# Banded attention in layer 1: softmax sums in eight tiles of 64 by 32, their reciprocal in three parts

## The chip, the core and the metric

The kernel runs on one core of a Trainium2 chip. A core has five engines that run side by side: TensorE (PE in the profile; its weight loads are shown apart as PEld), VectorE (DVE), ScalarE (ACT), GpSimd (POOL) and SyncE (SP), which here issues the transfers. The metric is the device time of one execution in microseconds, as the median of several runs. Lower is better.

## What is computed

Two layers follow each other on an image `x` of 128 rows of 256 tokens of 256 channels, all in fp32. Each normalizes by groups, attends within each row, and adds its input. Layer 0 has eight heads of 32 channels, a gate and a bias behind the softmax. The change lies in layer 1, which has four heads of 64 channels and lets a token see only the tokens at most 16 away:

```python
qkv = x2 @ w_in.T + b_in
q, k, v = map(heads, jnp.split(qkv, 3, axis=-1))        # 4 heads of 64 channels
scores = jnp.einsum('bhid,bhjd->bhij', q, k) / jnp.sqrt(D)
scores = jnp.where(jnp.abs(i - j) <= 16, scores, -jnp.inf)
attn = jax.nn.softmax(scores, axis=-1)
out = jnp.einsum('bhij,bhjd->bhid', attn, v)
y = out.reshape(...) @ w_out.T + b_out
```

## The kernel before

One image row of 256 tokens is a sample; there are S = 128 samples in 64 pairs. Layer 1 keeps channels on the partitions and tokens along the free side. The tokens are cut into NB = 4 blocks of KB = 64 keys; a block of keys meets a window of 96 queries at most. The four heads are numbered by `half` (0 or 1) and `j` (0 or 1). The keys of the heads of half 0 lie on partitions 0 to 63, those of half 1 on partitions 64 to 127 of the same tile, so that TensorE can be used as four tiles of 64 by 64: rows by `half`, columns by `j`.

The softmax isn't divided out before the product with v. The exponentials go into a banded tile `p`, and POOL adds its two rows of blocks into `zp` (L1085), in which the sum over the 64 partitions of a half is the softmax's sum of each of the 256 queries. `attend` (L1088 to L1122) does for a pair, sample r = 0 and then r = 1:

- 16 products of `p` with v into `av` (L1107), in tiles of 64 by 64;
- 4 products of `zp` with a matrix `place` into `zs` (L1117), also in tiles of 64 by 64. `place` has ones in 16 of its 64 columns, other ones for each half and sample, so that the sums of 2 halves and 2 samples gather on different groups of 16 partitions. Sample 0 starts the accumulation in PSUM and sample 1 ends it; each half has its own PSUM bank.

Each fp32 product shows in the profile as two matmuls (two passes). `sums` (L1124) then adds the two banks: ACT copies one (L1129), DVE adds the other (L1130). `inverse` takes the reciprocal on DVE (L1141) in two parts of 128 columns. `by_transfer` writes one row of each group of 16 partitions to DRAM (L1149, two transfers) and reads it back spread over 64 partitions each (L1153, two transfers) into `near`; SP issues all four. `divide` multiplies `av` by `near` on DVE (L1173), which gives `at`. The last two pairs use two products with `spread` (L1164) in place of the transfers.

Layer 1's loop runs over pairs i in an order written out by hand for all engines: scores of pair i; output transposes and stores of pair i - 3 (`finish`); `attend`, `sums` and the first part of `inverse` for pair i - 1; then `stretch(i + 1, i - 2)`, the projections; then normalization of pair i + 2 (on ACT; its helper also has SP issue the load of a later pair's `yg`), `divide(i - 1)`, the row sums of `at` on POOL, the least of the sums on DVE (`bounds`), and the values v of pair i + 1 (L1047).

`stretch` runs three streams at once: q and k of pair i + 1, and the output projection o of pair i - 2. Each has seven products n, made in the order 2, 1, 5, 6, 7, 4, 3 (a scheme with seven products in place of eight); `in_turn` (L687 to L700) goes round the three streams for each n. Behind each product the stream's bank is emptied (`take`): for q and k mostly by ACT (L666, L668), for o by DVE (L662), and the additions L675, L681, L685 by DVE. A stream has one PSUM bank, so its next product waits for the take. Behind product 1 of all three streams, `amid` puts the second part of the reciprocal and the transfers into the order.

Of the kernel before, what the change touches and what calls it, by code (L numbers as in the profile page):

```python
# [39 lines left out]
def conv_preact_kernel(  # L40
# [59 lines left out]
    def strip(a):  # L100
        return slice(B * a, B * (a + 1))
# [582 lines left out]
            elif n == 3:  # L684
                nc.vector.tensor_tensor(to[:, 2], ps[:, 1, :], self.mid, ALU.add)  # L685

    def in_turn(sevens, amid=lambda: None):  # L687


        for p in sevens:  # L690
            p.open()

            p.product(2, p.ps[:, 1, :], first=True)
            p.take(2)
        for n in (1, 5, 6, 7, 4, 3):
            for p in sevens:
                p.product(n)
                p.take(n)
            if n == 1:
                amid()  # L700

    def one_by_one(w, at, name, done):

# [19 lines left out]
    with ExitStack() as both:  # L723
# [20 lines left out]
        with ExitStack() as lay0:  # L744
# [140 lines left out]
            def stretch(names, i, s, rest=lambda: None):  # L885

                po = iter(())
                if s >= 0:
                    po = one_by_one(out_sb, st[s]["at"], f"po{s}", lambda ps: st[s].update(po=ps))
                if 2 * i >= S:  # L890
                    rest()
                    for _ in po:
                        pass
                    return
                f, g = (
                    Seven(row, quarters[w], xns[i], tss[i], f"{w}{i}", w, by_token=(w == "v")) for w in names
                )
                for w, p in zip(names, (f, g)):
                    res[w, i] = p.to
                two_of_them(row, f, g, f"{names}{i}", po, rest)  # L900
# [70 lines left out]
        with ExitStack() as lay:  # L971
# [4 lines left out]

            weights = [att.tile([P, 2, 2 * WROW], F32, name=f"1p{i}", bufs=1) for i in range(4)]

            place = att.tile([P, 2, D1], F32, name="place", bufs=1)
            nc.gpsimd.memset(place, 0.0)  # L980
            for half in range(2):
                for r in range(2):
                    c = 32 * half + 16 * r
                    nc.gpsimd.memset(place[KB * half : KB * (half + 1), r, c : c + 16], 1.0)

            spread = att.tile([P, 2, 2, P], F32, name="spread", bufs=1)
            for half in range(2):
                for r in range(2):
                    nc.gpsimd.tensor_copy(
                        spread[:, half, r].rearrange("p (j d) -> p j d", j=2),  # L990
                        ident[:, 32 * half + 16 * r :: D1].unsqueeze(2).to_broadcast([P, 2, D1]),
                    )
            xns, tss = {}, {}

# [26 lines left out]

            ats, ats_t, outputs, last_ots = {}, {}, {}, {}

            def stretch(i, j, amid=lambda: None):


                streams = [
                    Summed(row, quarters1[w], xns[i], tss[i], f"1{w}{i}", w, bias=bqk[:, 0:2] if w == "q" else None)
                    for w in "qk"
                ]  # L1030
                f, g = streams
                if j >= 0:
                    outputs[j] = Summed(row, quarters1["o"], ats[j], ats_t[j], f"1o{j}", "out", bias=bo_v, y=ygs[j])
                    streams.append(outputs[j])
                in_turn(streams, amid)
                for r in range(2):
                    st[2 * i + r].update(q=f.to[:, 2 * r : 2 * r + 2, :], k=g.to[:, 2 * r : 2 * r + 2, :])
# [50 lines left out]
            def attend(i):  # L1088

                if i < 0:  # L1090
                    return

                if i < S // 2 - 1:
                    av = ps_av.tile([P, 2, 2, R], F32, tag="av", name=f"1av{i}", bufs=1)
                    av = [av[:, half] for half in range(2)]
                else:
                    av = [proj_bank(f"1av{i}_{half}") for half in range(2)]
                zs = ps_av.tile([P, 2, 2, R], F32, tag="zs", name=f"1zs{i}", bufs=1)
                for r in range(2):
                    (p, zp), v = hd.pop(2 * i + r), st[2 * i + r]["v"]  # L1100
                    for b in range(NB):
                        for half in range(2):
                            for j in range(2):
                                keys, cols = slice(KB * half, KB * (half + 1)), slice(D1 * j, D1 * (j + 1))
                                q0, p0 = QLO[b], R * (b % 2) + QLO[b]

                                nc.tensor.matmul(  # L1107
                                    av[half][cols, r, q0 + QIN[b].start : q0 + QIN[b].stop],
                                    lhsT=v[keys, b, cols],
                                    rhs=p[keys, j, p0 + QIN[b].start : p0 + QIN[b].stop],  # L1110
                                    start=(r == 0 and b == 0), stop=(b == NB - 1),
                                    skip_group_check=True,
                                )
                    for half in range(2):
                        for j in range(2):
                            keys, cols = slice(KB * half, KB * (half + 1)), slice(D1 * j, D1 * (j + 1))
                            nc.tensor.matmul(  # L1117
                                zs[cols, half, 0, :], lhsT=place[keys, r, :], rhs=zp[keys, j, :],
                                start=(r == 0), stop=(r == 1),
                                skip_group_check=True,  # L1120
                            )
                hd["av", i] = (av, zs)  # L1122

            def sums(i):  # L1124
# [7 lines left out]
                near = att.tile([P, 2, 2, R], F32, tag="near", name=f"1near{i}", bufs=1)  # L1132
                hd["z", i] = (z, rz, near)

            def inverse(i, part):

                if i < 0:
                    return
                z, rz, _ = hd["z", i]
                cols = slice(P * part, P * (part + 1))  # L1140
                nc.vector.reciprocal(rz[:, cols], z[:, cols])  # L1141

            def by_transfer(i):

                if i < 0:
                    return
                _, rz, near = hd["z", i]
                for j in range(2):
                    nc.sync.dma_start(  # L1149
                        out=rz_far[i % 2, j], in_=rz[D1 * j : D1 * (j + 1)].rearrange("(n c) q -> n c q", c=16)[:, 0, :]  # L1150
                    )
                for j in range(2):
                    nc.sync.dma_start(  # L1153
                        out=near[D1 * j : D1 * (j + 1)].rearrange("p h r q -> p (h r q)"),
                        in_=rz_far[i % 2, j].rearrange("n q -> (n q)").partition_broadcast(D1),
                    )

            def by_product(i):

                _, rz, near = hd["z", i]  # L1160
                for half in range(2):
                    ps = proj_bank(f"1near{i}_{half}")
                    for r in range(2):
                        nc.tensor.matmul(ps[:, r, :], lhsT=spread[:, half, r], rhs=rz, start=True, stop=True)  # L1164
                    nc.scalar.copy(near[:, half], ps)

            def divide(i):
                if i < 0:
                    return
                ats[i] = row.tile([P, 4, R], F32, tag="at", name=f"1at{i}", bufs=2)  # L1170
                av = hd.pop(("av", i))[0]
                for half in range(2):
                    nc.vector.tensor_tensor(ats[i][:, half::2], av[half], hd["z", i][2][:, half], ALU.mult)  # L1173
                for r in range(2):
                    st[2 * i + r]["at"] = ats[i][:, 2 * r : 2 * r + 2, :]

# [63 lines left out]
            with tc.manual_schedule(engines={  # L1240
# [12 lines left out]
                for i in range(last):  # L1253
                    s = 2 * i
                    scores(s)
                    scores(s + 1)
                    finish(i - 3)
                    attend(i - 1)
                    sums(i - 1)
                    inverse(i - 1, 0)  # L1260

                    def amid():
                        inverse(i - 1, 1)
                        by_transfer(i - 1)

                    stretch(i + 1, i - 2, amid)
                    normal(i + 2, True)
                    divide(i - 1)
                    if 0 <= i - 1 < last - 2:
                        ats_t[i - 1] = row.tile([P, 4, R], F32, tag="att", name=f"1att{i - 1}", bufs=2)  # L1270
                        row_sums(ats_t[i - 1], ats[i - 1], nc.gpsimd)
                    bounds(i - 1)
                    values(s + 2)
                    values(s + 3)
# [15 lines left out]
                sums(last - 1)  # L1290
                for s in (S - 6, S - 5):
                    all_of(s)
                for part in range(2):
                    inverse(last - 1, part)
                by_product(last - 1)
                for s in (S - 6, S - 5):
# [1 line left out]
                attend(last)  # L1298
                sums(last)
                divide(last - 1)  # L1300
                for part in range(2):
                    inverse(last, part)
                all_of(S - 4)
                by_product(last)
# [214 lines left out]
```

## Time and profile before

| what | value |
|---|---|
| median of 3 runs | 3195.79 us (3195.11 to 3196.19) |
| the profiled execution | 3194.72 us, span from its first to its last instruction 3193.0 us |
| mean granted TensorE clock | 0.993 |
| busy PE / PEld | 3115.2 us (98%) / 2404.0 us (75%) |
| busy DVE / ACT / POOL | 2536.9 us (79%) / 1868.3 us (59%) / 1609.2 us (50%) |
| one pass of layer 1's loop | 16.79 us, PE's start of v to the next one |
| reciprocal of the sums, L1141, 128x128 | 947 ns, 124 times |
| products of the sums, L1117 | 1024 recorded matmuls |
| division, L1173 | 686 ns, waits 53.7 us in all for `1near` |

A span is divided among the engines by their busy time, but matmuls are pipelined and their ends are modelled: two that overlap are not each a cost, so PE's cost is read from the distance between starts. A line of a timeline gives start, length over all that were merged, engine, source line, operation, output and inputs, for a matmul the tile of the array (rows by columns) and the shapes, the count, and in brackets how long the engine had been idle and who ended that. DVE's instructions overlap by some 0.08 us when they follow each other without a wait.

### The profile page before, as it was taken

What the parts mean: (1) busy time and instruction counts of PE and PEld (TensorE: products, weight loads), DVE (VectorE), ACT (ScalarE), POOL (GpSimd) and SP (SyncE); (2) the same over time, 40 slices, a digit from 0 to 9 for tenths busy, and PEclk for the clock granted to TensorE, in tenths of its full rate; (3) what the DMA queues carried; (4) which work ended last, traced back from release to release, by engine and by line L of the source; (5) the groups of instructions that cost most, each with busy time, mean ns of one, the idle gap of its engine ahead of it and who ended that gap; (6) DMA issues with size and microseconds to landing.
All of it is one profiled execution on the core that took longest, in us unless ns stands there. A gap on an engine that the chain in (4) does not pass through costs nothing.

```text
span 3193.0 us, 87583 instructions
## 1 busy us (share of the span) xinstructions
PE 3115.2 (98%) x36859; PEld 2404.0 (75%) x36859; DVE 2536.9 (79%) x4076; ACT 1868.3 (59%) x4064; POOL 1609.2 (50%) x1653
## 2 busy tenths in 40 slices
PE   7889999999999999999999999999999999999997
PEld 4567777777777777777777777678888888888886
DVE  4669999999999999999999999946666666666665
ACT  4666666666666666666666666545555555555553
POOL 3034444444444444444444444266667666766674
PEclk9999999999999999999999999999999999999999
DMA  9931111111111111111111111014444434443443
GB/s 379 424 104 41 47 34 41 35 41 34 41 35 34 41 36 39 34 41 34 41 34 41 34 34 41 28 41 100 95 96 94 101 95 96 93 101 95 98 91 69
DMA packets 357104, 242.43 MB, mean 76 GB/s; under 512 B 276072, under 2 KB 342112, under 8 KB 350560
## 3 DMA queue, kind: packets, MB, share of 16 engines
q1 hardware_dynamic: 355808, 234.39, 26.9%
q8 instruction: 292, 4.78, 0.6%
q0 software_dynamic: 752, 2.36, 0.2%
q14 instruction: 108, 0.88, 0.1%
q10 hardware_dynamic: 144, 0.00, 0.0%
HBM read 169.09 MB, written 67.62 MB: 74 GB/s over the span
## 4 chain that ended last, share of the span: by engine, by line
PE 92%; DMA 4%; DVE 2%; ACT 1%; issue 0%; POOL 0%; SPq 0%; DVEq 0%; POOLq 0%; ACTq 0%
PE sim L784 9%; PE p1v L1047 7%; PE po L708 7%; PE bv L816 7%; PE av L816 7%; PE p1q L594 6%; PE p1o L594 6%; PE p1k L594 6%; PE pv L598 6%; PE pq L594 6%; PE pk L594 5%; PE pg L594 5%; PE zs L830 4%; PE 1sim L1068 3%; DMA pr<-in_L_conv_pair_repr_dram 3%; PE 1av L1107 2%
## 5 line engine op out<-in xcount | busy, mean ns | idle before, releaser
L797 ACT ACTIVATE ex<-sim 128x512 f32<-128x512 f32 x1024 | 548.0, 606 | 431.3 <-PE sim L784 431.3
L806 DVE TENSOR_TENSOR both<-ex 128x512 f32<-128x512 f32 x512 | 483.7, 983 | 72.3 <-ACT ex L797 72.2
L846 DVE RECIPROCAL d<-d 128x512 f32<-128x512 f32 x128 | 429.2, 3353 | 4.4
L611 POOL TENSOR_TENSOR v<-v,twovg 128x256 f32<-128x256 f32 x64 | 75.1, 1174 | 548.3 <-ACT twovg L630 548.3
L784 PE MATMUL sim<-q,k 32*128 32x256 f32 x4096 | 295.8, 401 | 1.1 <-ACT ex L797 1.1
L708 PE MATMUL po<-at,out_sb 128*128 128x256 f32 x1024 | 285.2, 382 | 4.0 <-DVE at L864 4.0
L784 PEld LDWEIGHTS sim<-q,k 32*128 32x128 f32 x4096 | 186.7, 185 | 102.4 <-issue 95.0
L816 PE MATMUL bv<-bias_sb,v 128*32 128x256 f32 x4096 | 244.5, 379 | 0.7 <-DVE t L861 0.7
L816 PE MATMUL av<-ex,v 128*32 128x256 f32 x4096 | 244.5, 379 | 0.0
L668 ACT ACTIVATE 1q<-p1q,bqk 128x256 f32<-128x256 f32 x192 | 90.9, 474 | 257.7 <-PE p1q L594 257.7
L1047 PEld LDWEIGHTS p1v<-w_in_t,1xn 128*64 128x64 f32 x4096 | 222.3, 137 | 21.5 <-PE p1k L594 20.2
L1047 PE MATMUL p1v<-w_in_t,1xn 128*64 128x128 f32 x4096 | 237.7, 274 | 0.3 <-POOL place L980 0.3
L1078 POOL TENSOR_TENSOR 1p<-1ex,seen 128x768 f32<-128x768 f32 x127 | 230.3, 1813 | 14.5 <-ACT 1ex L1076 14.5
L708 PEld LDWEIGHTS po<-at,out_sb 128*128 128x128 f32 x1024 | 186.0, 192 | 25.1 <-issue 4.3
L1130 DVE TENSOR_TENSOR 1z<-1zs,1z 128x256 f32<-128x256 f32 x64 | 27.2, 424 | 221.8 <-ACT 1z L1129 221.8
L816 PEld LDWEIGHTS bv<-bias_sb,v 128*32 128x32 f32 x4096 | 133.5, 110 | 88.3 <-issue 1.1
L816 PEld LDWEIGHTS av<-ex,v 128*32 128x32 f32 x4096 | 133.6, 110 | 87.5 <-issue 0.3
L611 POOL TENSOR_TENSOR q<-q,twoqk 128x256 f32<-128x256 f32 x64 | 47.3, 740 | 294.7 <-ACT twoqk L630 294.7
L568 POOL TENSOR_TENSOR 1ts<-1xn 128x256 f32<-128x256 f32 x64 | 46.8, 731 | 294.3 <-ACT 1xn L1008 294.3
L766 DVE TENSOR_SCALAR xn<-xt,mean,rstd 128x256 f32<-128x256 f32 x256 | 180.8, 745 | 0.0
L1085 POOL TENSOR_TENSOR 1zp<-1p 128x512 f32<-128x512 f32 x127 | 161.7, 1273 | 10.0
L1054 ACT COPY 1v<-p1v 128x512 f32<-128x512 f32 x128 | 75.1, 587 | 135.2 <-PE p1v L1047 131.8
(300 smaller groups left out, 8022.0 us busy)
## 6 DMA issues: line engine op xcount, KB each, us to landing
pr<-in_L_conv_pair_repr_dram SPq DMA_DIRECT2D x32, 1024.0 KB
xs<-in_x_dram SPq DMA_DIRECT2D x16, 2048.0 KB
x<-o SPq DMA_DIRECT2D x64, 512.0 KB
yg<-x SPq DMA_DIRECT2D x64, 512.0 KB
out_dram<-1o SPq DMA_DIRECT2D x256, 128.0 KB
xg<-in_x_dram SPq DMA_DIRECT2D x252, 128.0 KB
1near<-rz_far SPq DMA_DIRECT2D x124, 256.0 KB
rz_far<-1rz SPq DMA_DIRECT2D x124, 4.0 KB
```

The lines of the kernel that those rows point to most:

```text
L594: nc.tensor.matmul(out, lhsT=weights, rhs=moving, start=first, **flags)
L598: nc.tensor.matmul(out[:, cols], lhsT=moving[:, cols], rhs=weights, start=first and t2 == 0, **flags)
L708: nc.tensor.matmul(ps[:, m, :], lhsT=w[:, kt, m * P : (m + 1) * P], rhs=at[:, kt, :], start=(kt == 0), stop=(kt == 1),)
L766: nc.vector.tensor_scalar(xns[i][:, 2 * r + half, :], xt[:, half, :], mean0[:, half : half + 1], rstd0[:, half : half + 1], op0=ALU.subtra ...
L784: nc.tensor.matmul(sims[j][:, kt, :], lhsT=k[p0 : p0 + D0, 2 * r + half, kt * P : (kt + 1) * P], rhs=q[p0 : p0 + D0, 2 * r + half, :], sta ...
L797: nc.scalar.activation(ex[:, j], sims[j], AF.Exp, scale=1.0 / math.sqrt(D0))
L806: nc.vector.tensor_tensor(both[:, j : j + 2], ex[:, j : j + 2, 0, :], ex[:, j : j + 2, 1, :], ALU.add)
L816: nc.tensor.matmul(to[D0 * j : D0 * (j + 1), half, :], lhsT=v[:, 2 * r + half, c0 : c0 + D0], rhs=weights(4 * half + j, kt), start=(kt == ...
L846: nc.vector.reciprocal(d, d)
L1047: nc.tensor.matmul(ps[KB * half : KB * (half + 1), b, :], lhsT=xns[i][:, 2 * r + kt, KB * b : KB * (b + 1)], rhs=w_in_t[:, kt, 2 * C + P * ...
L1078: engine.tensor_tensor(p.rearrange("p j (r c) -> p (j r) c", c=WROW)[:, :, 0 : 2 * WSTEP] .rearrange("p r (t c) -> p r t c", c=WSTEP)[:, : ...
L1085: engine.tensor_tensor(zp, p[:, :, 0:R], p[:, :, R : 2 * R], ALU.add)
```

## The change

The sums: both samples' `zp` are kept until all products with v of the pair are in the queue, and then eight products follow, one for each half, head column j and sample, in tiles of 64 rows by 32 columns. Column strip 2 j + r takes sample r and column j, row half `half` takes the heads of that half, and each half writes its own bank. `place` needs no sample any more: 32 columns, 16 of them ones for each half. Nothing accumulates over the samples.

The order of the 16-partition groups is now (j, r, half) where it was (j, half, r); so `near` is read with the sample ahead of the half, and `spread` picks other rows.

The reciprocal: three parts of 64, 128 and 64 columns. The first stays behind `sums`, the second behind product 1 of the streams, and the third comes behind product 5, with the transfers after it.

```diff
-    def in_turn(sevens, amid=lambda: None):
+    def in_turn(sevens, amid=lambda n: None):
...
-            if n == 1:
-                amid()
+            if n in (1, 5):
+                amid(n)
...
-            place = att.tile([P, 2, D1], F32, name="place", bufs=1)
+            place = att.tile([P, B], F32, name="place", bufs=1)
             nc.gpsimd.memset(place, 0.0)
             for half in range(2):
-                for r in range(2):
-                    c = 32 * half + 16 * r
-                    nc.gpsimd.memset(place[KB * half : KB * (half + 1), r, c : c + 16], 1.0)
+                nc.gpsimd.memset(place[KB * half : KB * (half + 1), 16 * half : 16 * (half + 1)], 1.0)
...
-                        ident[:, 32 * half + 16 * r :: D1].unsqueeze(2).to_broadcast([P, 2, D1]),
+                        ident[:, B * r + 16 * half :: D1].unsqueeze(2).to_broadcast([P, 2, D1]),
...
+                zps = []
                 for r in range(2):
                     (p, zp), v = hd.pop(2 * i + r), st[2 * i + r]["v"]
+                    zps.append(zp)
...
+
+                for r in range(2):
                     for half in range(2):
                         for j in range(2):
-                            keys, cols = slice(KB * half, KB * (half + 1)), slice(D1 * j, D1 * (j + 1))
+                            keys = slice(KB * half, KB * (half + 1))
                             nc.tensor.matmul(
-                                zs[cols, half, 0, :], lhsT=place[keys, r, :], rhs=zp[keys, j, :],
-                                start=(r == 0), stop=(r == 1),
-                                skip_group_check=True,
+                                zs[strip(2 * j + r), half, 0, :], lhsT=place[keys, :], rhs=zps[r][keys, j, :],
+                                start=True, stop=True,
                             )
...
+            PARTS_Z = (slice(0, R // 4), slice(R // 4, 3 * R // 4), slice(3 * R // 4, R))
+
             def inverse(i, part):
...
-                cols = slice(P * part, P * (part + 1))
+                cols = PARTS_Z[part]
                 nc.vector.reciprocal(rz[:, cols], z[:, cols])
...
-                        out=near[D1 * j : D1 * (j + 1)].rearrange("p h r q -> p (h r q)"),
+                        out=near[D1 * j : D1 * (j + 1)].rearrange("p r h q -> p (r h q)"),
...
-                    nc.scalar.copy(near[:, half], ps)
+                    nc.scalar.copy(near[:, :, half], ps)
...
-                    nc.vector.tensor_tensor(ats[i][:, half::2], av[half], hd["z", i][2][:, half], ALU.mult)
+                    nc.vector.tensor_tensor(ats[i][:, half::2], av[half], hd["z", i][2][:, :, half], ALU.mult)
...
-                    def amid():
-                        inverse(i - 1, 1)
-                        by_transfer(i - 1)
+                    def amid(n):
+                        inverse(i - 1, 1 if n == 1 else 2)
+                        if n == 5:
+                            by_transfer(i - 1)
...
-                for part in range(2):
+                for part in range(3):
                     inverse(last - 1, part)
```

The last line also changes for the last pair in the same way.

More of the change, by code (lines that the diff above doesn't have):

```diff
@@ L1022, in conv_preact_kernel, with stretch @@
             ats, ats_t, outputs, last_ots = {}, {}, {}, {}
-            def stretch(i, j, amid=lambda: None):
+            def stretch(i, j, amid=lambda n: None):
                 streams = [
@@ L1300, in conv_preact_kernel @@
                 divide(last - 1)
-                for part in range(2):
+                for part in range(3):
                     inverse(last, part)
```

## The prediction

> **What bounds the kernel.** I read the chain that ended last first, to learn which engine sets the end.
>
> ```profile
> PE 92%; DMA 4%; DVE 2%; ACT 1%; issue 0%; POOL 0%; SPq 0%; DVEq 0%; POOLq 0%; ACTq 0%
> ```
>
> TensorE (PE) is the path, so an edit counts by what it takes from or adds to PE's own order; the rest counts only where PE comes to wait for it. Then PE's timeline of one steady pass of layer 1's loop (start, length, engine, line, operation):
>
> ```profile
> 2601.01 0.74 PE L1107 MATMUL 1av<-1p,1v 64*64 64x80 f32 x28
> 2601.55 0.38 PE L1117 MATMUL 1zs<-1zp,place 64*64 64x256 f32 x1
> ...
> 2601.98 0.81 PE L1107 MATMUL 1av<-1p,1v 64*64 64x80 f32 x29
> 2602.59 0.38 PE L1117 MATMUL 1zs<-1zp,place 64*64 64x256 f32 x1
> ...
> 2602.68 0.61 PE L1117 MATMUL 1zs<-1zp,place 64*64 64x256 f32 x7
> 2603.22 0.70 PE L594 MATMUL p1q<-1xn,w_in_t 128*128 128x256 f32 x2
> ```
>
> The sums stand twice in a pass, eight recorded matmuls each (four tiles, two passes of fp32 per product). From the first start of sample 0's sums (2601.55) to the first av of sample 1 (2601.98) PE advances 0.43 us: two rounds of 0.216, all four tiles side by side. So one set of sums costs PE 0.433 us. Passes repeat every 16.79 us.
>
> The price of a new tiling I take from layer 0, where 64x32 does not occur either, but 128x32 does:
>
> ```profile
> 1400.71 1.15 PE L784 MATMUL sim<-q,k 32*128 32x256 f32 x16
> 1401.79 1.07 PE L830 MATMUL zs<-both,ones 128*32 128x256 f32 x16
> 1402.67 1.91 PE L816 MATMUL bv<-bias_sb,v 128*32 128x256 f32 x32
> 1404.40 1.91 PE L816 MATMUL av<-ex,v 128*32 128x256 f32 x32
> 1406.24 1.15 PE L784 MATMUL sim<-q,k 32*128 32x256 f32 x16
> ```
>
> bv, with no change of tiling on either side, takes 1.73 us for eight rounds: 0.216 a round with four column tiles at work. av, the same eight rounds with a change behind it, takes 1.84: leaving costs some 0.1. zs takes 0.88 for four rounds (0.865), so entering 32-column tiles adds 0.02. Single starts in the trace say the same more finely: 0.09 us between the last product's end and the first start in the new tiling, then an extra 0.024 us on the first round in 32-column tiles, 0.052 in 64-column ones, 0.104 in whole-array ones.
>
> Last, all engines of the same pass, for the reciprocal:
>
> ```profile
> 2604.18 0.60 PE L594 MATMUL p1o<-1at,w_out_t 128*128 128x256 f32 x2
> 2604.22 0.95 DVE L1141 RECIPROCAL 1rz<-1z 128x128 f32<-128x128 f32 x1
> ...
> 2605.05 0.60 PE L594 MATMUL p1k<-1xn,w_in_t 128*128 128x256 f32 x2
> 2605.09 0.38 DVE L662 SCALAR_TENSOR_TENSOR 1o<-p1o,bo_v,yg 128x256 f32<-128x256 f32 x1
> ...
> 2605.52 0.30 PEld L594 LDWEIGHTS p1o<-1at,w_out_t 128*128 128x128 f32 x2 [0.28 <-DVE 1o L662]
> 2605.53 0.70 PE L594 MATMUL p1o<-1at,w_out_t 128*128 128x256 f32 x2
> ...
> 2606.06 0.59 PE L594 MATMUL p1q<-1ts,sums_1q 128*128 128x256 f32 x2
> ...
> 2608.90 0.49 DVE L662 SCALAR_TENSOR_TENSOR mid1o<-p1o,bo_v,yg 128x256 f32<-128x256 f32 x1 [0.86 <-PE p1o L594]
> ...
> 2614.83 1.29 DVE L1173 TENSOR_TENSOR 1at<-1av,1near 128x512 f32<-128x512 f32 x2 [1.58 <-DMA 1near<-rz_far]
> ```
>
> DVE sits in the first reciprocal until 2605.17 while stream o's product 2 is done at 2604.78. So DVE's take of it (L662) is late, and with it the weight load of o's product 1. Normal steps between streams are 0.432; here p1k to p1o is 0.48 and p1o to the next p1q 0.53. Over 61 passes the medians are 44 and 104 ns: 0.148 us lost per pass. The same stream loses only 44 ns at products 6 and 7, where DVE stands free when the product ends.
>
> **The change, part by part.**
>
> *Sums.* Removed: the sums of sample 0 amid the av products, 0.433 us a pair. Added: the tiling changes from 64x64 to 64x32 ahead of the one remaining set. The set itself stays two rounds if eight tiles work side by side. Four column tiles at once are shown at 0.216 a round (bv); two row halves writing two PSUM banks at once are shown by the sums of now; both together occur nowhere. I take two rounds. Bounds from these rows: 0.43 us (eight together) to 0.87 (four at a time, as now); the first, because each half of the demand is shown at full speed. The entry: last av start 2602.627 + 0.067 (80 columns) + 0.09, first round 0.240, second round 0.216, starts of eight tiles spread over 7 x 6.5 ns = 0.046 (layer 0's spacing), and then 0.306 from the last sums' start to p1q, as now. That puts p1q 0.162 us later than now, before the 0.433 is taken off. Bounds of this term: 0 (the array need not empty) and 0.26 (the dearest change in the trace, 128x32 to 32x128, 0.217, and the spread). Going from whole array to 128x64 keeps the row split and still costs 0.09 + 0.052 (p1o to p1v), so I keep 0.162. Net: 0.433 - 0.162 = 0.271 us, and all 64 pairs have it: **17.3 us**.
>
> The Trainium skill ("TensorEngine Tiling (Array Packing)", Tiling Modes, Key Properties) says that changing the tiling, not just the tile, drains the array, which speaks against this change; it gives no figure. The rows above show the drain as 0.09 us, 64 x 0.09 = 5.8 us; without the drain the gain would be that much more. The skill ("TensorE: Matmul & The Clock Gate", Part 3) spaces packed tiles by about 4 ns instead of the 6.5 seen here; by it the sum would be 64 x 7 x 2.5 ns = 1.1 us better.
>
> *Reciprocal.* Two rows give its cost: 128x512 at 3353 ns (L846) and 128x128 at 947 ns (L1141), so 6.27 ns a column and 145 ns fixed. 64 columns: 546 ns. The first part now ends at 2604.22 + 0.55 = 2604.77, when o's product 2 has just ended (2604.78). So L662 starts near 2604.82 instead of 2605.09 and the stall should shrink to what products 6 and 7 show: 148 to 44 ns, **0.104 us x 61 = 6.3 us**. Bounds: nothing gained (0), all of it (9.0). The second part keeps its 128 columns and its place. The third, 0.55 us, falls behind L662 of product 5 (ends 2608.04) and ahead of L662 of product 6 (starts 2608.90, after 0.86 us of idleness): it fits with 0.3 us to spare, so nobody behind it on DVE waits. Were the cover gone, each 0.1 us would cost 6 us.
>
> *Transfer.* The two small stores and two broadcasts of the reciprocals leave 0.9 us later (reciprocal's end 2607.54 to about 2608.45). On SP's queue only the load of yg (2610.43) follows them; it is used a pass later. Who waits: the division (L1173), and behind it on DVE the least of z, four transposes and so the output stores, all with over 1.5 us of idle DVE before the next sums; POOL's row sums of 1at (POOL idles 4.8 us a pass); and PE's next av, which overwrites what the division reads. I took the time from the division's end to the next av in 65 passes: median 2.28 us, lowest 0.98. The later start takes 0.91 of it and PE's shorter pass 0.10: 1.27 is left in the median, about 0 in the one tightest pass. Cost: 0 to 0.1 us in all.
>
> *Rest.* The new order inside near and spread changes only which 256-column runs are read; the division already writes with a stride. Bound 0 either way to one instruction's fixed part, hidden under DVE's idleness. The two last pairs do three reciprocal parts on the path: 2 x 0.145 = 0.3 us more.
>
> Sum: 17.3 + 6.3 - 0.3 = 23.3 us. The profiled execution took 3194.72 us (span 3193.0), so it becomes 3171.4; the median of the three runs, 3195.79, lies 1.07 above that execution, so **3172.5 us**, 0.73% less. This kernel can be told from no change beyond about 0.2%, 6.4 us.
>
> **Rivals.**
> A, the forecast: 3172.5. For it: every part is a row's duration. Chance 0.77.
> D, the sums gain but the stall stays (DVE's take is late for another reason, for instance its operands from PE): 17.0 us, 3178.8. Against it: products 6 and 7 have the same pattern and lose less. Chance 0.07.
> C, the change does not do what it says: eight tiles run only four at a time. Then 0.433 is not saved, the tiling change is paid: 64 x 0.162 - 6.3 + 0.3 = +4.4 us, 3200.2, within 0.2%. For it: no row shows eight. Chance 0.09.
> B, the other side: the transfer comes too late and av waits for the division. It decides from 1.27 us of extra landing time; the gain is eaten at 1.27 + 0.38 = 1.65 us. If the later broadcasts meet the yg load or the stores and take 2 us longer than their median 6.6 us from reciprocal to division, each pass waits 0.73 us: 61 x 0.73 - 23.3 = +21 us, 3217. Against it: the order on the queue is unchanged, and the longest of 65 transfers took 7.92 us. Chance 0.07.
>
> **How the numbers follow.** A and D make 0.84 faster; C 0.09 the same; B 0.07 slower. The range covers A and D with the bounds of their terms. High: tiling change at 0.26 and the stall unchanged, 64 x 0.173 = 11 us less the 0.3, 3185 and a bit: 3186. Low: tiling change at 0 and the stall wholly gone, 27.7 + 9.0 - 0.3 = 36.4, 3159.4: 3160.
>
> **What would show it.** In the changed profile: one run of sixteen 1zs matmuls in 64*32, with the second eight starting 0.24 us after the first (C: four starts, then four more 0.2 us on); about 0.1 us ahead of them without a start; p1k to p1o near 0.43 and p1o to p1q near 0.48 at product 1 (D: 0.48 and 0.53); the reciprocal's parts near 546, 947, 546 ns; the wait of the division for 1near grown from 0.9 to some 1.8 us, and no av held by the division (B: av behind L1173). Passes should repeat every 16.79 - 0.375 = 16.42 us. Eight tiles at less than full speed, or an entry dearer than 0.26 us, would make the prediction wrong.

## The result and the profile after

The changed kernel takes 3170.74 us (3170.26 to 3175.28, four runs) against 3195.99: a ratio of 0.9927, with an interval of 0.9915 to 0.9939. The forecast was 3172.5.

The profiled execution is the slowest of the four, 3175.28 us with a span of 3173.6. Its chain of waits still runs through TensorE:

```profile
PE 91%; DMA 5%; DVE 2%; ACT 1%; issue 0%; POOL 0%; SPq 0%; DVEq 0%; POOLq 0%; ACTq 0%
```

The span fell by 19.4 us, but layer 1 fell by more. Before PE's first product of v the new profile is 3.5 us longer (2085.5 to 2089.1 us; layer 0, which the change does not touch, already ends that much later, and DMA's share of the chain has risen). From there to the end it is 1107.5 us before and 1084.5 after: 23.0 us less. The prediction's sum was 23.3.

PE's timeline of one pass (start, length, engine, line, operation):

```profile
2609.92 1.42 PE L1107 MATMUL 1av<-1p,1v 64*64 64x80 f32 x63
2611.27 0.66 PE L1119 MATMUL 1zs<-1zp,place 64*32 64x256 f32 x16
2611.86 0.70 PE L594 MATMUL p1q<-1xn,w_in_t 128*128 128x256 f32 x2
2612.40 0.59 PE L594 MATMUL p1k<-1xn,w_in_t 128*128 128x256 f32 x2
```

There is one set of sums, sixteen recorded matmuls in 64*32. The single starts show eight within 0.047 us (2611.270 to 2611.317), and the second eight 0.240 us after the first: all eight tiles work side by side. The last av starts at 2611.111, so its 0.067 us and 0.092 us of emptiness lie ahead of the sums. From the last sums' start to p1q it is 0.306 us, as before.

All engines of the same pass, for the reciprocal:

```profile
2612.93 0.55 DVE L1144 RECIPROCAL 1rz<-1z 128x64 f32<-128x64 f32 x1
...
2613.46 0.48 DVE L662 SCALAR_TENSOR_TENSOR 1o<-p1o,bo_v,yg 128x256 f32<-128x256 f32 x1
...
2613.69 0.59 PE L594 MATMUL p1k<-1xn,w_in_t 128*128 128x256 f32 x2
...
2614.00 0.32 PEld L594 LDWEIGHTS p1o<-1at,w_out_t 128*128 128x128 f32 x2
...
2614.12 0.59 PE L594 MATMUL p1o<-1at,w_out_t 128*128 128x256 f32 x2
...
2614.56 0.59 PE L594 MATMUL p1q<-1ts,sums_1q 128*128 128x256 f32 x2
...
2616.45 0.54 DVE L1144 RECIPROCAL 1rz<-1z 128x64 f32<-128x64 f32 x1
...
2617.39 0.48 DVE L662 SCALAR_TENSOR_TENSOR mid1o<-p1o,bo_v,yg 128x256 f32<-128x256 f32 x1 [0.40 <-PE p1o L594]
```

The steps from p1k to p1o and on to p1q are 0.43 and 0.44 us: the stall of product 1 is gone. The third part of the reciprocal fits between two takes, with 0.40 us of idleness left. Later in the pass, DVE's own timeline:

```profile
2623.57 1.29 DVE L1176 TENSOR_TENSOR 1at<-1av,1near 128x512 f32<-128x512 f32 x2 [1.82 <-DMA 1near<-rz_far]
```

The division waits 1.82 us for near. The usual pass is now 16.37 us, 0.42 less; 14 of 61 passes are longer, by 4.3 us together (3 passes and 1.3 us before). In ten of the 14, 3.1 us together, the first av starts 0.15 us behind the division's end, which is the least distance in any trace here: PE waits for the division. The other four, 1.2 us, are held ahead of other products, as the three before are.

### The profile page after: what moved, and what is told of

Same layout as the page of the kernel before. It is cut to its first block, busy times and chain, and to the rows that moved or that the text cites. A ratio compares the mean times of both kernels' runs of the same rounds, so it can differ in the third digit from the quotient of the medians.

```text
span 3173.6 us, 87645 instructions
## 1 busy us (share of the span) xinstructions
PE 3097.4 (98%) x36859; PEld 2384.0 (75%) x36859; DVE 2558.2 (81%) x4140; ACT 1870.3 (59%) x4064; POOL 1613.4 (51%) x1651
## 4 chain that ended last, share of the span: by engine, by line
PE 91%; DMA 5%; DVE 2%; ACT 1%; issue 0%; POOL 0%; SPq 0%; DVEq 0%; POOLq 0%; ACTq 0%
PE sim L784 9%; PE p1v L1045 7%; PE po L708 7%; PE av L816 7%; PE bv L816 7%; PE p1q L594 6%; PE pv L598 6%; PE p1o L594 6%; PE pq L594 6%; PE p1k L594 6%; PE pk L594 5%; PE pg L594 5%; DMA pr<-in_L_conv_pair_repr_dram 4%; PE zs L830 4%; PE 1sim L1066 3%; PE 1av L1107 3%
## 5 line engine op out<-in xcount | busy, mean ns | idle before, releaser
L1176 DVE TENSOR_TENSOR 1at<-1av,1near 128x512 f32<-128x512 f32 x128 | 82.6, 686 | 148.6 <-DMA 1near<-rz_far 116.7
```

## The experiments

Times are medians, compared with the kernel before on the same chip (3193.8 to 3195.1). "Usual pass" is the median distance between PE's starts of v in the profiled execution; "lengthened" are the passes more than 0.05 us above it.

### The eight tiles alone

```diff
-            PARTS_Z = (slice(0, R // 4), slice(R // 4, 3 * R // 4), slice(3 * R // 4, R))
+            PARTS_Z = (slice(0, P), slice(P, R))
...
-            if n in (1, 5):
+            if n == 1:
...
-                        inverse(i - 1, 1 if n == 1 else 2)
-                        if n == 5:
-                            by_transfer(i - 1)
+                        inverse(i - 1, 1)
+                        by_transfer(i - 1)
...
```

The loops over the parts for the last pairs also go back to two.

> The eight tiles alone, with the reciprocal in two parts of 128 and the transfers behind product 1, as before the change. Theory (the sums and the stall behind the first reciprocal are separate terms): 64 x 0.271 = 17.3 us less than before, near 3178.7 us; passes of 16.79 - 0.27 = 16.52 us; at product 1 of stream o the steps of 0.48 and 0.53 us stay; the division still waits some 0.9 us for near and no pass is lengthened by it. Rival (the gain is the reciprocal's, the sums give nothing): no change, 3196.

Measured: 3182.27 us, ratio 0.9956 (0.9939 to 0.9973); usual pass 16.59 us, 3 lengthened passes (0.4 us). The gain is in the sums as well, but 0.20 us a pass and not 0.27. All engines of a pass show why:

```profile
2614.10 0.37 ACT L1130 COPY 1z<-1zs 128x256 f32<-128x256 f32 x1 [0.94 <-PE 1zs L1119]
...
2615.84 0.38 DVE L662 SCALAR_TENSOR_TENSOR 1o<-p1o,bo_v,yg 128x256 f32<-128x256 f32 x1
...
2616.27 0.30 PEld L594 LDWEIGHTS p1o<-1at,w_out_t 128*128 128x128 f32 x2 [0.35 <-DVE 1o L662]
```

The weight load now waits 0.35 us for L662, where it was 0.28. The median stall of product 1 is 0.219 us, where it was 0.148. The added 0.071 us come from further up: ACT starts its copy of the sums 508 ns after the last sum's start, where it was 440, in this kernel and in the changed one alike. DVE's add and the reciprocal follow as much later. With four tiles of 64 by 32 at a time (the run "One change of tiling more") it is 443 ns, so the delay goes with the set of eight and not with the narrow tiles; why is open. 16.79 - 0.27 + 0.07 = 16.59.

### The reciprocal in three parts alone

The kernel before, with the diff's edits to `in_turn`, `inverse` and `amid` and three parts for the last pairs only.

> The reciprocal in three parts and the later transfers alone; sums in two sets of 64 by 64 as before. Theory: the stall at product 1 goes wholly, 61 x 0.148 = 9.0 us, and the late transfers give back some 3 us as in the changed kernel: near 3190; passes of 16.64 us where no transfer is late. Rival (the transfers are late only because the sums have become shorter): no lengthened pass, 3187.

Measured: 3188.63 us, ratio 0.9978 (0.9968 to 0.9987); usual pass 16.64 us, 12 lengthened passes (3.1 us). The stall goes wholly, and passes are lengthened without the shorter sums, so the later transfer does it. The two parts alone bring 12.8 and 6.4 us, together 19.2, less than the 25.3 of the whole change: alone, the tiles make the stall worse by 61 x 0.071 = 4.3 us, and together the short first part takes that away. The 1.8 us then left are within what these medians can tell.

### The order of the sums alone

```diff
+                zps = []
                 for r in range(2):
...
+                    zps.append(zp)
...
+                for r in range(2):
                     for half in range(2):
                         for j in range(2):
...
-                                zs[cols, half, 0, :], lhsT=place[keys, r, :], rhs=zp[keys, j, :],
+                                zs[cols, half, 0, :], lhsT=place[keys, r, :], rhs=zps[r][keys, j, :],
```

> Sums still in tiles of 64 by 64 and two sets, only moved behind both samples' products with v; all else as before. Theory: what counts is the number of rounds and of tiling changes, not where the sums stand: no change, 3196 within 2 us. Rival (part of the gain comes from no longer breaking up the products with v, whose four tiles run shifted against each other by some 0.1 us around the sums): up to 64 x 0.1 = 6 us less, 3190.

Measured: 3195.29 us, ratio 1.0001 (0.9992 to 1.0011); usual pass 16.79. Where the sums stand is worth nothing. PE's timeline has both sets of 64*64 behind each other:

```profile
2603.31 0.38 PE L1120 MATMUL 1zs<-1zp,place 64*64 64x256 f32 x1
2603.34 0.24 PE L1109 MATMUL 1av<-1p,1v 64*64 64x80 f32 x3
2603.41 1.04 PE L1120 MATMUL 1zs<-1zp,place 64*64 64x256 f32 x15
2604.38 0.70 PE L594 MATMUL p1q<-1xn,w_in_t 128*128 128x256 f32 x2
```

### One change of tiling more

The changed kernel, with sample 0's products of 64 by 32 amid the products with v:

```diff
-
-                for r in range(2):
                     for half in range(2):
                         for j in range(2):
                             keys = slice(KB * half, KB * (half + 1))
```

> The changed kernel, but with sample 0's four products of 64 by 32 back amid the products with v, so that four tiles run at a time and the tiling changes twice more a pair. Theory: 0.433 us for the second set, 0.114 to enter and 0.142 to go back to 64 by 64, 0.69 us a pair, 44 us more than the changed kernel's 3171: 3215. Rival (a change of the column split alone empties nothing): 0.433 us a pair, 28 us more: 3199.

Measured: 3214.01 us, ratio 1.0058 (1.0042 to 1.0075); usual pass 17.07 us, 0.70 more than the changed kernel's. PE's timeline:

```profile
2607.51 0.93 PE L1107 MATMUL 1av<-1p,1v 64*64 64x80 f32 x31
2608.37 0.64 PE L1117 MATMUL 1zs<-1zp,place 64*32 64x256 f32 x8
2608.94 0.84 PE L1107 MATMUL 1av<-1p,1v 64*64 64x80 f32 x32
2609.70 0.64 PE L1117 MATMUL 1zs<-1zp,place 64*32 64x256 f32 x8
2610.27 0.70 PE L594 MATMUL p1q<-1xn,w_in_t 128*128 128x256 f32 x2
```

A set is two rounds whether four tiles work or eight, so half the tiles idle here. From a set's start to the next work is 0.57 us, and 0.433 of it are rounds; the rest belongs to the way in and out. Changing only the column split, from 64 by 64 to 64 by 32 and back, costs 0.70 - 0.433 = 0.27 us, where the other tilings' rows gave 0.256. It also shows what the kernel would be if narrow tiles replaced the wide ones without filling the array: slower than before.

### The changed kernel again

> The changed kernel once more, beside the kernels that change its transfers. Theory: 3170 to 3172, passes of 16.37 us and some ten to twenty passes lengthened, 3 to 5 us in all. No rival.

Measured: 3169.30 us, ratio 0.9923 (0.991 to 0.9937), 6 lengthened passes (0.8 us). Beside a later pair of kernels:

> The changed kernel a third time, as the measure for the kernel with yg ahead beside it: 3168 to 3172, some passes lengthened, 1 to 5 us in all.

Measured: 3173.09 us, ratio 0.9931 (0.9917 to 0.9944), 15 lengthened passes (4.2 us). The usual pass is 16.37 us each time. Between the profiled execution with few lengthened passes (span 3167.5 us) and the other two (3171.9 and 3173.6), these passes are the larger part of the difference: 3.4 of 4.4 and 3.5 of 6.1 us.

### One store in place of two

```diff
-                for j in range(2):
-                    nc.sync.dma_start(
-                        out=rz_far[i % 2, j], in_=rz[D1 * j : D1 * (j + 1)].rearrange("(n c) q -> n c q", c=16)[:, 0, :]
-                    )
+                nc.sync.dma_start(
+                    out=rz_far[i % 2].rearrange("j n q -> (j n) q"),
+                    in_=rz.rearrange("(n c) q -> n c q", c=16)[:, 0, :],
+                )
```

> The changed kernel with the two small stores of the reciprocals made one, which saves one issue of some 0.55 us on SP ahead of the broadcasts. Theory (the lengthened passes come from av waiting for a late division, that from near): near lands 0.55 us sooner, so lengthened passes nearly go, 2 to 4 us less than the changed kernel: 3167 to 3169. Rival (the lengthened passes have another cause, such as instruction loads): no change from the changed kernel.

Measured: 3169.30 us, ratio 0.992 (0.9907 to 0.9934), the same as the changed kernel beside it; 9 lengthened passes (2.6 us). The theory's step was wrong: the broadcasts were not waiting for SP's second issue. They start 1.72 us after the reciprocal's end with one store and 1.66 with two, since they wait for the store to land. This run says nothing on the cause of the lengthened passes.

### The load of yg ahead of the transfers

```diff
                     def amid(n):
+                        if n == 1:
+                            load1(i + 3)
```

> The changed kernel with the load of yg issued behind product 1, ahead of the reciprocals' transfers, in place of behind them. Theory (the broadcasts take 7.5 us instead of 6.5 in some passes because the 512 KB of yg, issued right behind them, share the transfer engines): the time from the reciprocal to the division falls to about 6.5 us in nearly all passes, lengthened passes go, 2 to 4 us less than the changed kernel. Rival (other traffic, or the broadcasts alone): the two kinds of passes stay, no change; or yg now stands in front of them and makes it worse, some 60 x 0.3 us, 18 us more.

Measured: 3167.67 us, ratio 0.9916 (0.9903 to 0.993); no lengthened pass. With the changed kernel beside it a second time:

> The load of yg ahead of the reciprocals' transfers, a second time. Theory: again no lengthened pass and 1 to 3 us less than the changed kernel beside it. Rival (the difference of 1.6 us in the first try was chance): no difference, or lengthened passes as many as there.

Measured: 3167.40 us, ratio 0.9914 (0.99 to 0.9928), one lengthened pass (0.1 us). SP's timeline of the changed kernel, and then of this one:

```profile
2617.03 1.09 SPq L1152 DMA_DIRECT2D rz_far<-1rz  x2
2618.66 1.12 SPq L1156 DMA_DIRECT2D 1near<-rz_far  x2
2619.87 0.53 SPq L741 DMA_DIRECT2D yg<-x  x1
```

```profile
2625.53 0.52 SPq L741 DMA_DIRECT2D yg<-x  x1
2629.56 1.09 SPq L1152 DMA_DIRECT2D rz_far<-1rz  x2
2631.18 1.12 SPq L1156 DMA_DIRECT2D 1near<-rz_far  x2
```

The load waits little in that order (25.0 us in 48 passes in the first try, 20.4 in 40 in the second, never over 1.4), so SP issues it close behind the output stores, in the pass shown 4 us ahead of the reciprocals' transfers. In the changed kernel a median of 173 packets of yg start within the stretch of the broadcasts' own packets (100 in the kernel before); here, in 61 of 62 passes, none do. The median time from the reciprocal to the division falls from 7.1 to 6.5 (first try) and 6.7 us (second), and the lengthened passes go both times. So the theory holds as far as av's wait goes. But the slow kind stays: with no yg beside them the broadcasts' packets still take 2.3 to 4.2 us; what the slow ones meet stands in the next section. In total time the two tries gave 1.6 and 5.7 us against the changed kernel beside them, up to 0.18%; the intervals overlap, so that this version is faster than the changed one is shown by the passes rather than by the times.

Both edits together:

> One store and yg ahead of the transfers, together. Theory: no lengthened pass at all: 3171 - 4 = 3167. Rival: as for yg ahead alone.

Measured: 3167.78 us, ratio 0.9917 (0.9903 to 0.993), no lengthened pass: nothing beyond yg ahead alone.

### The transfers later still

The price of rival B, with the third part behind product 7:

```diff
-            if n in (1, 5):
+            if n in (1, 7):
...
-                        if n == 5:
+                        if n == 7:
```

> The changed kernel with the third part of the reciprocal, and so the transfers, behind product 7 in place of product 5, in another idle stretch of DVE: 2.62 us later. Theory (the margin between the division's end and the next av is some 1.4 us where the transfer takes its shortest 6.4 us, and what is later than that PE waits in full): every pass lengthened by 2.62 - 1.42 = 1.2 us at least and about 0.6 more where the broadcasts are slow, 61 x 1.2 to 1.8: 73 to 110 us more than the changed kernel, 3245 to 3280. Rival (the margin is wider because something else than av's wait decides): under 30 us more.

Measured: 3271.31 us, ratio 1.0252 (1.0237 to 1.0268); usual pass 17.84 us, 1.47 more than in the changed kernel. The waits of PE (in all, times, longest), and a pass:

```profile
PE 1av L1107 <- DVE 1at L1176: 76.3, 55, 2.6
```

```profile
2617.60 1.29 DVE L1176 TENSOR_TENSOR 1at<-1av,1near 128x512 f32<-128x512 f32 x2 [5.36 <-DMA 1near<-rz_far]
...
2619.04 1.44 PE L1107 MATMUL 1av<-1p,1v 64*64 64x80 f32 x64 [2.04 <-DVE 1at L1176]
```

av starts 0.15 us after the division's end in every pass. Of 2.62 us of delay the margin hid 1.15, and PE waited for all that was left.

## Why the prediction was right, and where it was not

**The sums**: right in mechanism and size. The usual pass fell by 0.42 us. 0.148 of it is the stall, so the sums gave 0.272; the forecast was 0.271. (The second round's 0.216 us stands in the prediction's list, but is rightly not in its 0.162: the 0.306 us run from the starts of that round.) Rival C (four at a time) fell with the first profile. That the tiling change was rightly charged is shown by the kernel with one change more: 0.70 us a pass measured, 0.69 worked out from layer 0's rows. This is also the run on the drain of which the Trainium skill ("TensorEngine Tiling (Array Packing)", Tiling Modes, Key Properties) speaks: without a drain it would have cost 0.43. Neighbouring tiles start 6.7 ns apart, not the about 4 of the skill's "TensorE: Matmul & The Clock Gate", Part 3.

**The stall**: right mechanism, a term sized too small. "148 to 44 ns" was taken from products 6 and 7; measured is 148 to 0, 9.0 us in place of 6.3. Rival D fell. Products 6 and 7 still lose their 44 ns in the changed kernel, though L662 ends 0.18 us ahead of the due product there as it does at product 1. So the likeness that the prediction drew does not hold, and what those two wait for is not settled: their weight loads start 0.12 us after L662's end, that of product 1 starts 0.05 us after it, and the profile names no releaser.

**The copy of the sums**, costed at nothing, starts 68 ns later behind the set of eight tiles. Alone this costs 0.071 us a pass (4.3 us); in the whole change the shorter first part of the reciprocal covers it.

**The transfer**: "Cost: 0 to 0.1 us in all" is the step that failed. In the profiled execution the lengthened passes take 3.0 us more than before (4.3 against 1.3), and the ten in which av waits for the division make 3.1. The margin was worked out rightly for the transfers of before (1.3 us in the median, of which av's 0.15 us behind the division cannot be used; behind product 7 it hid 1.15), but their spread was taken to stay. It did not: the median from reciprocal to division went from 6.6 to 7.1 us and the longest from 7.9 to 8.4 (62 transfers each; the prediction counts 65). In the changed kernel the median from the division's end to av is 0.92 us, and in eleven passes it is the bare 0.15. So rival B's mechanism does act, in a sixth of the passes: 3 us, where the rival reckoned with 61 x 0.73 = 44.5.

**The third part** of the reciprocal (546 ns forecast, 547 measured) fits its gap, and the tail of the last pairs is unchanged (42.8 us from the last start of v to the end, before and after; 42.4 in the other two profiled executions of the changed kernel), so the 0.3 us that the extra part was to cost there cannot be told from what varies.

The sum: 62 x 0.272 in the loop, 9.0 for the stall and 3.0 back is 22.9 us, against 23.0 measured in layer 1. The total came out near the forecast partly because two errors, 2.7 us too little for the stall and 3.0 us too little for the transfer, cancel.

**What the slow transfers meet** can be read from the packets in the traces. Beside the data, the profile's page lists 292 packets of 16 KB on a queue of the kind "instruction" (q8); one takes some 1.1 us. In 28 of the changed kernel's 62 transfers such a packet starts 0.5 to 2.0 us after the broadcasts' first packet. These broadcasts take 3.1 to 4.3 us, and the median from reciprocal to division is 7.7 us. The other 34 take 2.4 to 3.2 us and 6.6 in the median, as in the kernel before, where none of the 62 meets an instruction packet at that place. All eleven passes with the bare 0.15 us are among the 28. Behind product 7, 2.6 us later again, only 6 of 62 meet one so. All packets in the stretch of the slowest broadcasts of the changed kernel (4.32 us), and in that of the fastest (2.40 us; packets, MB, share of the DMA engines):

```profile
q1 hardware_dynamic: 654, 1.02, 90.7%
q8 instruction: 1, 0.02, 1.7%
```

```profile
q1 hardware_dynamic: 209, 0.57, 94.2%
```

So the start 0.9 us later brought the broadcasts to where instructions are loaded in nearly half of the passes, and the load of yg, issued right behind them, adds to it: with yg ahead 29 of 62 still meet an instruction packet and take 3.1 to 4.2 us, but the median from reciprocal to division is then 7.0 and 7.1 us (two tries) in place of 7.7, and the margin hides it. For yg this is shown by a change of the kernel; for the instruction packets it is a coincidence in the traces, since no run moved them.

## What to carry to other kernels

Count a group of small products by rounds of the array and by changes of tiling, from distances between starts: filling eight tiles in place of four halves the rounds, and must pay for the way in (here 0.433 us won, 0.16 paid). Half-filled narrow tiles with an extra change of tiling lose. When a transfer is moved later into a margin, its times at the old place need not hold at the new one: look there at what is issued right behind it on the same queue and at what the instruction queue moves; a load that nobody needs soon can go ahead of it for nothing.

## What the runs showed of the hardware

A set of eight 64 by 32 fp32 tiles with 256 columns runs its two passes in 0.240 + 0.216 us, as fast as four tiles of 128 by 32 in layer 0. Going from 64 by 64 to 64 by 32 and back costs 0.27 us though the row split stays. ACT, which waits for such a set of eight, starts 508 ns after the last start, in place of 440 behind four tiles of 64 by 64 and 443 behind four of 64 by 32, with the same recorded length of the last matmul (376 ns). Broadcasts of 128 packets in which a 16 KB instruction packet starts after 0.5 to 2.0 us took 3.1 to 4.3 us in the changed kernel, the others 2.4 to 3.2.
